# Step sizes of a selective-scan kernel: products of both halves in one instruction, both stores in slot 1

## The chip, the core and the metric

The kernel runs on one core of a Trainium2 chip. The core has TensorE (PE in the profile; PEld is its weight loads), VectorE (DVE), ScalarE (ACT), GpSimd (POOL), and SyncE (SP), which here only issues DMAs. The metric is the device time of one execution in microseconds. Three executions of the kernel before took 18705.48 to 18734.97 us, median 18718.93.

## What is computed

The input is 8 images of 48 x 48 pixels and 96 channels. Four layers follow each other, each in the form x = x + layer(group_norm(x)). Layer 0 and layer 3 are two-dimensional selective scans (`ss2d`), layer 1 is a spectral up- and downsampling with a small network between, layer 2 is a selective scan along lines (rows and columns, forwards and backwards). The scan that layers 0, 2 and 3 share, cut to what matters:

```python
delta = softplus(dts + dt_bias)                        # step sizes, 192 channels
def step(h, inp):                                      # along the sequence
    dl, u, B, C = inp
    dA = exp(dl[..., None] * A)                        # 16 states for each channel
    h = h * dA + (dl * u)[..., None] * B[:, None, :]
    return h, einsum('bdn,bn->bd', h, C)
```

Each layer scans every image in four directions (`k`). In layers 0 and 3 a sequence is all 48 x 48 pixels. In layer 2 each row or column of 48 is a sequence of its own. The product `dl * u` is what the change is about: it is called the step size product below.

## The kernel before, in words

The 192 channels are two halves of 96 (`DH`). An image and direction is cut into five blocks of rows, four of 480 pixels and one of 384 (`BLKS`). There are 160 blocks (8 images, 4 directions, 5 blocks) in each of the three scan layers.

For each block a first stage (`stage1`) makes u, the step sizes dt and the step size products du on 96 partitions. They stand in one SBUF tile, `dds`, as [96, half, dt or du, columns]. The pool has one such buffer. The scan itself works on 128 partitions, each a pair of 32 channels and 4 states, so dt and du have to be repeated. This goes through DRAM: `store_dd` (line 437, one DMA of 360 KB for a half) writes them to DRAM, and `load_dd` (line 219, one DMA of 1440 KB for a half) reads them back with each row going to four partitions. B and C take the same way: `bcl` is stored as `bcd` (line 812 in lines, 658 in `ss2d`) and read by `load_bc` (line 231, 480 KB each, four for a block, seven buffers). All these DMAs are issued by SP, in order; a DMA whose wait is not over holds up all that stand behind it.

A block of the scan has eight slots, two in each of four turns. In a turn DVE does three scans (line 298) and up to two products of du and B (line 266); POOL does the rest of those products (line 266) and the products of the states with C (line 304). ACT makes the exponentials (line 290) and copies B to PSUM for DVE (`copy_b`, line 247, one PSUM buffer). PE sums over the states (lines 320 to 326). Half 0 of du is needed first by the product for slot 0, which DVE does in the fourth turn of the block before.

The order on each engine is the order in which the program records instructions, which is written out by hand in `scans`. The first-stage steps of a block are put at slots before it: `stage1` returns a table of slot offsets, and `plan` adds to it the start of the block two before the one they are for. `aside(at)` runs at each slot: first the loads of the next block (`LOAD_BC` = slots 2, 3, 6, 7; `LOAD_DD` = slot 3 for half 0 and slot 5 for half 1), then one step of other work, then the first-stage steps of that slot. In the lines layer the table has the convolution at offsets 3 and 4, u at 6, `bcl` at 7, the softplus and the store of `bcd` at 8 (`s6`), the step size products at 9 (`s7`), the store of half 0 at 10 (`s8`) and of half 1 at 11. Offsets 8 to 11 are slots 0 to 3 of the block before the one they are for. In `ss2d` the products stand at offset 7 and the stores at 8 and 9, that is, slots 0 and 1.

So in the lines layer SP issues, for each block: `bcd` store (slot 0), `bc` load (slot 2), store of half 0 (slot 2), `bc` load, load of half 0 and store of half 1 (slot 3), load of half 1 (slot 5), two `bc` loads (slots 6 and 7). Below, store 0 and store 1, load 0 and load 1 are those of the two halves.

`make_du` makes the step size product of one half on POOL (line 452). It then marks the ends of sequences: in the lines layer by a memset of dt at each line's first pixel (line 455), one for each half; in `ss2d` by two memsets over both halves (lines 459 and 460), made with half 0.

Of the kernel before, what the change touches and what calls it, by code (L numbers as in the profile page):

```python
# [23 lines left out]
SEG = 48  # L24
# [15 lines left out]
FAR = 1e30  # L40
# [17 lines left out]
def rows(t, n):  # L58

    return t[:, :n].rearrange("p (r s) -> p r s", s=SEG)  # L60
# [37 lines left out]
def vss_stack_kernel(ctx: ExitStack, tc: tile.TileContext, i: dict, out: bass.AP):  # L98
    nc = tc.nc
# [336 lines left out]
    def store_dd(b, half):  # L436
        nc.sync.dma_start(b.dd[half].rearrange("j (g m) -> g j m", g=3), b.dds[:, half].rearrange("p t m -> p (t m)"))

    def sizes(b, half):

        return [b.dds[:, half, n, b.at] for n in range(2)]

    def make_room(b, pools):
        b.room = pools["dds"].tile([DH, LEAD + 4 * WMAX], F32, tag="dds", name="dds")
        b.dds = b.room[:, LEAD:LEAD + 4 * b.m].rearrange("p (h t m) -> p h t m", h=2, t=2)

    def make_du(b, half, u):


        n = b.n  # L450
        dt, du = sizes(b, half)
        nc.gpsimd.tensor_mul(rows(du, n), rows(dt, n), u)  # L452
        if b.m == b.n:
            at = SEG - 1 if b.rev else 0
            nc.gpsimd.memset(rows(dt, n)[:, :, at:at + 1], FAR)
        elif half == 0:

            far = b.dds[:, :, :, b.came:] if b.back else b.room[:, :4 * b.m].rearrange("p (u m) -> p u m", m=b.m)[:, :, :LEAD + 1]
            nc.gpsimd.memset(b.dds[:, :, :, 0:1] if b.back else b.dds[:, :, :, b.goes:], 0.0)
            nc.gpsimd.memset(far, FAR)  # L460


    def ss2d(l, xin, xout, b0=0):
# [169 lines left out]
        def stage1(b):  # L633
            n = b.n
            u = b.view(us[b.job], dirs[b.k][0])
            got = {}

            def raw(half):
                got["p"] = ps("s1", 1)
                nc.tensor.matmul(got["p"][:DH, :n], lhsT=dtw[2 * NS:, b.k, half, :], rhs=b.bcl[2 * NS:, :n],  # L640
                                 start=True, stop=True)

            def biased(half):
                nc.scalar.activation(sizes(b, half)[0], got["p"][:DH, :n], AF.Identity,  # L644
                                     bias=w[f"{l}_dtb"][:, b.k, half:half + 1])

            def s0():
                got["p"] = ps("s1", 1)
                for half in range(2):
                    nc.tensor.matmul(got["p"][:NBC, :n], lhsT=w[f"{l}_xp"][:, b.k, half, :], rhs=u[:, half],  # L650
                                     start=(half == 0), stop=(half == 1))

            def s1():
                b.bcl = pools["bcl"].tile([NBC, BMAX], F32, tag="bcl", name="bcl")
                nc.scalar.copy(b.bcl[:, :n], got["p"][:NBC, :n])

            def s3():
                nc.sync.dma_start(b.bcd, b.bcl[:2 * NS, :n])
                raw(0)

            def s4():
                make_room(b, pools)
                biased(0)
                raw(1)

            def s6():
                both = b.dds[:, :, 0, b.at]
                nc.scalar.activation(both, both, AF.Softplus)  # L668

            def du():  # L670
                for half in range(2):
                    make_du(b, half, u[:, half])

            def store(half):
                return lambda: store_dd(b, half)

            return {-1: s0, 1: s1, 3: s3, 4: s4, 5: lambda: biased(1), 6: s6, 7: du,
                    NG: store(0), NG + 1: store(1)}

# [27 lines left out]
    def lines(xin, xout):  # L707
# [24 lines left out]
        for k in range(NK):  # L732
            nc.vector.tensor_mul(taps[:, k], taps[:, k], wl["l2_inu"][:, k].unsqueeze(1).to_broadcast([DH, 4, 2 * DH]))
            for half in range(2):
                nc.scalar.activation(diag[:, k, half, :], wc["ident"], AF.Identity, scale=w["l2_d"][:, k, half:half + 1])

                p = ps("s1", 2)
# [12 lines left out]
        def shift(t, dy, dx):  # L750

            at = (pad + dy) * step + pad + dx
            return t[:, at:at + H * step].rearrange("p (h w) -> p h w", w=step)[:, :, :W]
# [10 lines left out]
        def stage1(b):  # L764
            n = b.n
            col, rev = dirs[b.k]
            xp = xpads[b.job % 2]
            got = {}

            def shifted(off):  # L770
                v = shift(xp, off, 0).rearrange("p h w -> p w h") if col else shift(xp, 0, off)
                return v[:, b.r0:b.r0 + b.nr, :]

            def conv(half):
                def run():
                    got["u", half] = ps("s1", 2)
                    for tap in range(4):
                        off = tap - 3 if not rev else 3 - tap
                        at = ((b.k * 4 + tap) * 2 + half) * DH
                        nc.tensor.matmul(got["u", half][:, :n], lhsT=flat[:, at:at + P],  # L780
                                         rhs=shifted(off), start=(tap == 0), stop=(tap == 3))
                return run

            def s2():
                b.ub = up.tile([DH, 2, BMAX], F32, tag="ub", name="ub")
                for half in range(2):
                    nc.scalar.activation(b.ub[:, half, :n], got["u", half][:DH, :n], AF.Silu,
                                         bias=w["l2_cb"][:, b.k, half:half + 1])

            def s2s3():  # L790
                s2()
                s3()

            def s3():
                got["p"] = ps("s1", 2)
                for half in range(2):
                    nc.tensor.matmul(got["p"][:NBC, :n], lhsT=w["l2_xp"][:, b.k, half, :], rhs=b.ub[:, half, :n],
                                     start=(half == 0), stop=(half == 1))

            def s4():  # L800
                b.bcl = pools["bcl"].tile([NBC, BMAX], F32, tag="bcl", name="bcl")
                nc.scalar.copy(b.bcl[:, :n], got["p"][:NBC, :n])  # L802

            def s5():
                s4()
                for half in range(2):
                    got[half] = ps("s1", 2)
                    nc.tensor.matmul(got[half][:DH, :n], lhsT=dtw[2 * NS:, b.k, half, :], rhs=b.bcl[2 * NS:, :n],  # L808
                                     start=True, stop=True)

            def s6():
                nc.sync.dma_start(b.bcd, b.bcl[:2 * NS, :n])
                make_room(b, pools)
                for half in range(2):
                    nc.scalar.activation(sizes(b, half)[0], got[half][:DH, :n], AF.Softplus,  # L815
                                         bias=w["l2_dtb"][:, b.k, half:half + 1])

            def s7():
                for half in range(2):
                    got["z", half] = ps("s1", 2)  # L820
                    nc.tensor.matmul(got["z", half][:DH, :n], lhsT=w["l2_inz"][:, b.k, half * DH:(half + 1) * DH],  # L821
                                     rhs=shifted(0)[:C], start=True, stop=True)
                for half in range(2):
                    make_du(b, half, rows(b.ub[:, half], n))

            def s8():
                b.zb = up.tile([DH, 2, BMAX], F32, tag="zb", name="zb", bufs=2)
                for half in range(2):
                    nc.scalar.activation(b.zb[:, half, :n], got["z", half][:DH, :n], AF.Silu)
                store_dd(b, 0)  # L830

            return {3: conv(0), 4: conv(1), 6: s2s3, 7: s5, 8: s6, 9: s7, 10: s8, 11: lambda: store_dd(b, 1)}

        def opening(b, half):
            return diag[:, b.k, half, :], b.ub[:, half, :b.n]
# [42 lines left out]
        for _ in front(0):  # L878
            pass
        scans(dirs, range(NK), True, ON_POOL_L2, a, pools, ps, stage1, opening, done, side, tail)  # L880
        stack.close()

# [287 lines left out]
```

## Time and profile before

| | |
|---|---|
| median of 3 executions | 18718.93 us |
| the profiled execution | 18722.42 us |
| its span, first to last instruction | 18720.7 us |
| DVE busy | 16219.3 us (87%) |
| POOL busy | 15238.6 us (81%) |
| PE busy | 14799.0 us (79%) |
| ACT busy | 13661.6 us (73%) |
| DMA, mean | 152 GB/s |
| step size products (line 452), 480 columns, `ss2d` | 512 of 1237 ns |
| the same, lines | 256 of 1031 ns |

The layers follow each other in time: the first `ss2d` up to about 5.5 ms, the spectral layer to about 7.0 ms, the lines layer from there to about 13.2 ms (its first step size product starts at 7070.7 us, its last at 13195.7), and the second `ss2d` to the end. Shares of busy time over the whole span mix these. In the stretch 1000 to 5300 us (`ss2d`) DVE is busy 4134.6 us of 4300 and POOL 4021.2; in 7300 to 12300 (lines) DVE 4463.6 of 5000 and POOL 4086.2; in 13500 to 18300 (`ss2d`) DVE 4611.1 of 4800 and POOL 4487.5.

A line of the timeline has the start in us, the duration in us, the engine, the source line, the operation, what is written and read, the shape, how many instructions were merged into the line, and in brackets the idle time before it and what ended it. SPq is SP's queue: its lines are the issues of DMAs, not their transfers.

### The profile page before, as it was taken

The page shows a single profiled execution, that of the slowest core. Times are in us where ns is not written, and L with a number is a line of the kernel's source. Part 1 is how long each engine was busy: PE and PEld are TensorE (multiplying, and loading weights), DVE is VectorE, ACT ScalarE, POOL GpSimd, SP SyncE. Part 2 cuts the span into 40 slices and gives each one's busy share as a digit, 9 for nine tenths or more (in the row PEclk, how much of TensorE's full clock was granted, in tenths as well). Part 3 has the DMA queues.
Part 4 walks back from the last instruction along what each step waited for, and adds up shares of the span by engine and source line. Part 5 has one row for each costly group of instructions (what it writes and reads, how often), then busy time and mean ns, then how long its engine had stood idle before and what let it go on. Part 6 is the DMA issues. An engine that isn't in the chain of part 4 may idle for free.

```text
span 18720.7 us, 168607 instructions
## 1 busy us (share of the span) xinstructions
PE 14799.0 (79%) x53500; PEld 4319.5 (23%) x53500; DVE 16219.3 (87%) x10329; ACT 13661.6 (73%) x20342; POOL 15238.6 (81%) x8639
## 2 busy tenths in 40 slices
PE   6777777777778887887888878878777777777777
PEld 1211211212215552222222222221121121121221
DVE  7999999999992218889898888888799999999998
ACT  6877877887772227777777777777687788778776
POOL 7999999999980008888888888888799999999998
PEclk7876787777767778888888888888677778778776
DMA  4544544544544334444444444343454554554444
GB/s 139 174 173 166 175 171 165 178 170 165 176 148 55 46 60 144 147 146 149 148 147 148 146 151 148 142 150 135 144 172 170 172 171 168 171 172 170 169 172 147
DMA packets 768455, 2836.52 MB, mean 152 GB/s; under 512 B 235724, under 2 KB 298668, under 8 KB 640926
## 3 DMA queue, kind: packets, MB, share of 16 engines
q1 hardware_dynamic: 767558, 2825.75, 45.0%
q8 instruction: 418, 6.85, 0.1%
q14 instruction: 479, 3.92, 0.1%
HBM read 2377.32 MB, written 448.17 MB: 151 GB/s over the span
## 4 chain that ended last, share of the span: by engine, by line
POOL 29%; DVE 16%; DMA 16%; PE 15%; issue 14%; ACT 9%; SPq 1%; POOLq 0%; DVEq 0%; ACTq 0%
POOL dbu L304 20%; DVE dbu L298 10%; DMA dd<-dds 8%; POOL dbu L266 6%; DMA bc<-bcd 6%; DVE dbu L266 4%; ACT ps_da L290 4%; PE ps_y L324 2%; POOL dds L452 2%; PE ps_h L1010 2%; PE ps_s L780 2%; PE ps_y L1023 2%; ACT L290 1%; PE ps_side L515 1%; PE ps_a L1000 1%
## 5 line engine op out<-in xcount | busy, mean ns | idle before, releaser
L298 DVE TENSOR_TENSOR_SCAN dbu<-ps_da,dbu 128x968 f32<-128x968 f32 (+3 forms) x5760 | 11814.6, 2074 | 615.1 <-ACT ps_da L290 511.7
L304 POOL TENSOR_TENSOR dbu<-dbu,bc 128x1440 f32<-128x1440 f32 (+1 forms) x3840 | 10062.3, 2633 | 1549.8 <-DVE dbu L298 1485.6
L290 ACT ACTIVATE ps_da<-dd,w_l_a 128x484 f32<-128x484 f32 (+3 forms) x11520 | 7429.8, 649 | 2970.4 <-DVE dbu L298 2732.3
L324 PE MATMUL ps_y<-dbu,w_red 128*32 128x480 f32 (+1 forms) x23040 | 4855.5, 736 | 2059.7 <-POOL dbu L304 2037.3
L326 PE MATMUL ps_y<-dbu,w_red 128*32 128x480 f32 (+1 forms) x7680 | 4814.4, 736 | 0.0
L266 DVE TENSOR_TENSOR dbu<-dd,ps_b 128x962 f32<-128x962 f32 (+5 forms) x2880 | 3831.1, 1330 | 387.8 <-ACT ps_b L247 353.1
L266 POOL TENSOR_TENSOR dbu<-dd,bc 128x481 f32<-128x481 f32 (+5 forms) x2240 | 3911.1, 1761 | 245.4 <-DMA bc<-bcd 136.7
L324 PEld LDWEIGHTS ps_y<-dbu,w_red 128*32 128x32 f32 x23040 | 743.5, 124 | 6084.7 <-POOL dbu L304 4390.8
L247 ACT COPY ps_b<-bc 128x482 f32<-128x482 f32 (+3 forms) x2720 | 1450.8, 533 | 463.4 <-DMA bc<-bcd 345.4
L780 PE MATMUL ps_s<-xpad,w_l_cw 128*128 128x480 f32 (+1 forms) x2560 | 1748.0, 835 | 2.2 <-ACT xpad L146 1.9
L515 PE MATMUL ps_side<-xpad,w_l_cw 128*128 128x480 f32 (+1 forms) x2880 | 1575.3, 676 | 17.7 <-ACT u L528 12.7
L290 ACT ACT_TABLE_LOAD x986 | 1265.0, 1283 | 17.4
L135 POOL MEMSET w_l_cw<- 128x1760 f32 (+1 forms) x3 | 5.8, 1941 | 1338.8 <-DVE x L990 1333.3
L320 PE MATMUL ps_y<-ysum,w_ident 96*96 96x480 f32 (+1 forms) x960 | 747.1, 867 | 285.7 <-ACT ysum L692 285.7
L452 POOL TENSOR_TENSOR dds<-dds,u 96x480 f32<-96x480 f32 (+1 forms) x640 | 764.7, 1195 | 207.2 <-ACT dds L668 181.6
L640 PE MATMUL ps_s<-bcl,dtw 6*96 6x480 f32 (+1 forms) x1280 | 867.0, 765 | 65.1 <-ACT dds L644 57.7
L650 PE MATMUL ps_s<-u,w_l_xp 96*38 96x480 f32 (+1 forms) x1280 | 843.4, 790 | 20.9 <-ACT z L530 17.9
L808 PE MATMUL ps_s<-bcl,dtw 6*96 6x480 f32 (+1 forms) x640 | 459.1, 859 | 500.1 <-ACT bcl L802 500.1
L515 PEld LDWEIGHTS ps_side<-xpad,w_l_cw 128*128 128x128 f32 x2880 | 581.7, 225 | 1067.7 <-issue 928.3
L780 PEld LDWEIGHTS ps_s<-xpad,w_l_cw 128*128 128x128 f32 x2560 | 513.9, 206 | 1070.0 <-issue 964.6
L326 PEld LDWEIGHTS ps_y<-dbu,w_red 128*32 128x32 f32 x7680 | 682.8, 124 | 0.0
L821 PE MATMUL ps_s<-xpad,w_l_inz 96*96 96x480 f32 (+1 forms) x640 | 504.0, 921 | 63.8 <-ACT dds L815 48.2
(147 smaller groups left out, 11829.0 us busy)
## 6 DMA issues: line engine op xcount, KB each, us to landing
dd<-dd SPq DMA_DIRECT2D x512, 1452.0 KB
bc<-bcd SPq DMA_DIRECT2D x1536, 480.0 KB
dd<-dd SPq DMA_DIRECT2D x256, 1440.0 KB
dd<-dds SPq DMA_DIRECT2D x512, 363.0 KB
dd<-dd SPq DMA_DIRECT2D x128, 1164.0 KB
bc<-bcd SPq DMA_DIRECT2D x384, 384.0 KB
dd<-dds SPq DMA_DIRECT2D x256, 360.0 KB
dd<-dd SPq DMA_DIRECT2D x64, 1152.0 KB
```

What stands on the lines that cost most here:

```text
L247: nc.scalar.copy(bps[t][:, :bcs[t][0].shape[1]], bcs[t][0])
L266: engine.tensor_mul(o, du, by.unsqueeze(1).to_broadcast([P, hi - lo, by.shape[1]]))
L290: nc.scalar.activation(da[:, at:at + b.m], b.got[half][:, u % 3, 0, :], AF.Exp, scale=a[:, b.k, ci:ci + 1])
L298: nc.vector.tensor_tensor_scan(db, da, db, 0.0, ALU.mult, ALU.add)
L304: nc.gpsimd.tensor_mul(h, h, bcs.pop(2 * t + sub)[1].unsqueeze(1).to_broadcast([P, 3, n]))
L324: nc.tensor.matmul(y[32 * g:32 * g + 32, :n], lhsT=wc["red"][:, :32], rhs=hc[:, g, b.at], start=False, stop=(slot == 3))
L326: nc.tensor.matmul(y[DH:, :n], lhsT=wc["red"][:, 32:], rhs=hc[:, 2, b.at], start=(slot == 0), stop=(slot == 3))
L452: nc.gpsimd.tensor_mul(rows(du, n), rows(dt, n), u)
L515: nc.tensor.matmul(pu[:, :n], lhsT=flat[:, at:at + P], rhs=xpad[:, r0 + dy:r0 + dy + nr, dx:dx + W], start=(tap == 0), stop=(tap == 8))
L640: nc.tensor.matmul(got["p"][:DH, :n], lhsT=dtw[2 * NS:, b.k, half, :], rhs=b.bcl[2 * NS:, :n], start=True, stop=True)
L650: nc.tensor.matmul(got["p"][:NBC, :n], lhsT=w[f"{l}_xp"][:, b.k, half, :], rhs=u[:, half], start=(half == 0), stop=(half == 1))
L780: nc.tensor.matmul(got["u", half][:, :n], lhsT=flat[:, at:at + P], rhs=shifted(off), start=(tap == 0), stop=(tap == 3))
```

## The change

`make_du` no longer takes a half. It multiplies both halves in one POOL instruction over [96, 2, rows, 48], in all three scan layers. In the lines layer the memset that marks the sequence starts becomes one for both halves as well; in `ss2d` the two memsets now follow the one product, where they stood between the two. In the lines layer both stores go to offset 9, right behind the products: SP issues them ahead of the `bc` loads of slots 2 and 3. The step `s8` keeps the gate's activation alone, and offset 11 is gone. In `ss2d` the stores stay at offsets 8 and 9.

```diff
-    def make_du(b, half, u):
-        n = b.n
-        dt, du = sizes(b, half)
-        nc.gpsimd.tensor_mul(rows(du, n), rows(dt, n), u)
+    def make_du(b, u):
+        dt, du = [b.dds[:, :, n, b.at].rearrange("p h (r s) -> p h r s", s=SEG) for n in range(2)]
+        nc.gpsimd.tensor_mul(du, dt, u)
         if b.m == b.n:
             at = SEG - 1 if b.rev else 0
-            nc.gpsimd.memset(rows(dt, n)[:, :, at:at + 1], FAR)
-        elif half == 0:
+            nc.gpsimd.memset(dt[:, :, :, at:at + 1], FAR)
+        else:
...
             def du():
-                for half in range(2):
-                    make_du(b, half, u[:, half])
+                make_du(b, u)
...
-                for half in range(2):
-                    make_du(b, half, rows(b.ub[:, half], n))
+                make_du(b, b.ub[:, :, :n].rearrange("p h (r s) -> p h r s", s=SEG))
+                for half in range(2):
+                    store_dd(b, half)
 
             def s8():
...
-                store_dd(b, 0)
...
-            return {3: conv(0), 4: conv(1), 6: s2s3, 7: s5, 8: s6, 9: s7, 10: s8, 11: lambda: store_dd(b, 1)}
+            return {3: conv(0), 4: conv(1), 6: s2s3, 7: s5, 8: s6, 9: s7, 10: s8}
```

## The prediction

> **What bounds the kernel now.** I read the stretches by stage first, then the chain of waits and SP's waits inside the lines stage, then one block of that stage on SP, POOL and DVE. The two `ss2d` stages keep DVE 96% and POOL 93 to 94% busy (4134.6 and 4021.2 of 4300 us between 1000 and 5300), the lines stage only 89% and 82% (4463.6 and 4086.2 of 5000 us between 7300 and 12300): it waits for something else. This is its chain, and the largest row of SP's waits in that stretch:
>
> ```profile
> by line: DMA dd<-dds 21.3%; DMA bc<-bcd 14.4%; issue 8.7%; DVE dbu L298 8.5%; PE ps_s L780 5.9%; ACT ps_da L290 5.4%; POOL dbu L304 4.6%; DVE dbu L266 3.2%; PE ps_y L324 3.1%; PE ps_s L852 2.4%; DMA x<-x 2.3%; ACT L290 2.1%; POOL dbu L266 2
> ```
>
> ```profile
> SPq L219 <- DMA dd<-dds: 2487.9, 263, 11.3
> ```
>
> Every one of the 263 loads of step sizes waits, 9.5 us on average, for its own store to land. One block on SP's queue, and what came of it on DVE and POOL:
>
> ```profile
> 8999.86 0.31 SPq L812 DMA_DIRECT2D bcd<-bcl  x1
> 9001.50 0.51 SPq L231 DMA_DIRECT2D bc<-bcd  x1
> 9008.11 0.74 SPq L437 DMA_DIRECT2D dd<-dds  x1
> 9008.90 0.54 SPq L231 DMA_DIRECT2D bc<-bcd  x1
> 9019.06 0.51 SPq L219 DMA_DIRECT2D dd<-dd  x1
> 9019.67 0.73 SPq L437 DMA_DIRECT2D dd<-dds  x1
> 9031.00 0.53 SPq L219 DMA_DIRECT2D dd<-dd  x1
> 9031.58 1.24 SPq L231 DMA_DIRECT2D bc<-bcd  x2
> ```
>
> ```profile
> 9026.54 1.62 DVE L266 TENSOR_TENSOR dbu<-dd,ps_b 128x1440 f32<-128x1440 f32 x1
> ...
> 9039.10 1.66 DVE L266 TENSOR_TENSOR dbu<-dd,ps_b 128x1440 f32<-128x1440 f32 x1 [3.12 <-ACT ps_b L247]
> ```
>
> ```profile
> 9006.88 1.03 POOL L452 TENSOR_TENSOR dds<-dds,ub 96x480 f32<-96x480 f32 x1
> 9007.97 0.11 POOL L455 MEMSET dds<- 96x10 f32 x1
> 9008.03 1.03 POOL L452 TENSOR_TENSOR dds<-dds,ub 96x480 f32<-96x480 f32 x1
> ...
> 9045.68 0.86 POOL L452 TENSOR_TENSOR dds<-dds,ub 96x384 f32<-96x384 f32 x1
> ```
>
> Store 0 goes out at 9008.11, load 0 at 9019.06, store 1 behind it, load 1 at 9031.00, and only then the last two loads of `bc`. The first of them lands at 9038.42 (by the trace's semaphore updates), ACT copies it, and DVE's slot-2 product starts at 9039.10 after 3.12 us idle. From there 6.58 us run to the next block's products. So the cycle is 1.23 (product to store 0) + 30.31 (store 0 to that landing) + 0.68 + 6.58 = 38.80 us, the whole spacing. Over 124 steady 480-column blocks the spacing is 38.68 on average (37.6 to 40.3), over the 32 short ones 34.77.
>
> **The change in the lines stage.** SP's order becomes `bcd`, store 0, store 1, `bc`, `bc`, load 0, load 1, `bc`, `bc`. The built order confirms this, so "it does not do what it says" is no rival. `ss2d` already issues in nearly this order, and shows the prices:
>
> ```profile
> 3097.35 2.23 SPq L437 DMA_DIRECT2D dd<-dds  x2
> 3099.68 3.13 SPq L231 DMA_DIRECT2D bc<-bcd  x2
> 3107.18 0.51 SPq L219 DMA_DIRECT2D dd<-dd  x1
> ...
> 3112.14 0.52 SPq L219 DMA_DIRECT2D dd<-dd  x1
> ```
>
> Store 0 lands 9.8 us after its issue (load 0 goes out the moment it does), store 1 4.9 us later. The `bc` loads land at 16.1 and 17.3, load 0 at 20.8 us after store 0's issue; load 1 and the next `bc` at 24.4 and 25.5. Over 193 such full blocks load 0 lands at 20.4 to 22.9 us, mean 21.06; over 53 short ones at 18.0 in the median. Today in lines that is 17.5 (16.1 short). The reason is in what the queue does while a store runs alone:
>
> ```profile
> 9013.50:9017.50 4.00, 3.93 (x8) 1.39 (x9) 4.00 (x4) 3.94 (x7) 4.00 (x3) 1.00 0.17 59
> ```
>
> The last two columns are the share of the 16 DMA engines and GB/s: 0.17 is under three engines. The second store queues behind the first there, the two `bc` loads behind both, and load 0's part behind all four. [...]
>
> - *Product to store 0:* two 480-column products become one of 960. By POOL's rows (480: 1035 ns, 960: 1884, 1440: 2738) an element costs 1.77 ns and an instruction 0.18 us, so 1.88; with the gap, the memset and the issue (0.06 + 0.11 + 0.03) store 0 goes out 2.08 us after the product starts, not 1.23. [...]
> - *Load 0 to the next block's first DVE product:* 2.08 + 20.9 (a little under 21.06, since a store is 360 KB here and 363 there) + 0.1 = 23.1 us after the product starts. Today that DVE product comes at 21.0 on average, for other reasons (load 0 landed 2.3 earlier): a new stall of about 2 us.
> - *From there to the next block's step size product:* today 17.66 on average, with the `bc` stall in it. That stall goes: `bc` would land at 2.08 + 25.5 = 27.6 and be wanted at 23.1 + 9.4. Without waits it is 9.5 (smallest seen to the slot-2 product) + 6.6 = 16.1.
> - *Spacing:* 23.1 + 16.1 = 39.2 against 38.68: +0.52 x 128 blocks = +67 us. For load 0 at 20.4 and 16.0 it is 38.6 (-13 us); for 16.93, the median of the 42 blocks that have no `bc` stall today, 40.0 (+170 us).
> - *Short blocks:* 1.74 + 18.0 + 0.1 = 19.8, and the product comes at 20.3 today anyway: 0, at most +0.3 x 32 = 10.
> - *What queues behind the stores:* the first `bc` load moves from 5.4 us before the product to behind both stores and lands at about 18.4. Its ACT copy (today at 16.4) comes 2 us later; what hides that is load 0, which comes later still. If load 0 came early, this copy would be next, at about 19.
> - *POOL's own saving here* (one fixed part, a memset, a gap; some 0.3 us a block) costs and gives nothing: POOL waits 709.5 us for DVE's scans in this stretch. PE, ACT and DVE get the same instructions in the same order.
>
> **The change in ss2d.** Only the merge. A block saves one fixed part, 0.18 us; the two memsets stay. POOL's lines hold 32.2 + 9.5 + 2.6 = 44% of the chain there, so of 320 x 0.18 = 58 us I take 26; the ends are 0 (DVE is the bound: it waits for POOL in about 36 of 4300 us) and 58. Store 0 goes out 0.85 to 1.25 us later, since it now waits for both halves. In the block above load 0 lands at 3118.11 and the DVE product that needs it starts at 3129.55, so 11 us hide that: 0.
>
> **Sum.** 67 - 26 = +41 us. The profiled execution took 18722.4 (span 18720.7, 1.7 around it), 3.5 above the median 18718.9; so 18763 there, 18760 as a median. What can be told from no change here is about 0.2%, 37 us.
>
> **The rivals.**
> - *The wait moves and costs more* (chance 0.20): after the later DVE product the path takes 16.93, as in the 42 rows without `bc` stall, because the scan after it waits 1.07 us for ACT, and ACT for PE's second convolution. +170 - 26: 18865. For it: nearly all those rows. Against: in them the convolution ends 5 us after that product, and with the product 2 us later it should end in time.
> - *Faster* (0.12): load 0 comes as early as today, because the second store and the two `bc` loads do not hold its share up. Then the product stays at 21.0 and only the `bc` stall goes: 21.0 + 16.93 = 37.9, -0.75 x 128 = -96, with the merge -122: 18597. It decides at load 0 landing 20.4 us after store 0; later is slower. For it: that is only half a microsecond from my price. Against: of 193 blocks in `ss2d` none is below 20.36.
> - *The two parts cancel* (0.11): POOL's saving counts in full (-58) and load 0 is at the early end (+20): 18680.
> - *My forecast* (0.57): 18760, its own range 18710 to 18810.
>
> Slower by over 0.2%: 0.28 of the forecast and the first rival, 0.48. Within: 0.27 + 0.08 = 0.35. Faster: 0.02 + 0.12 + 0.03 = 0.17. The range 18650 to 18900 leaves out the faster rival and little else: low is both favourable ends together (-13 - 58), high the first rival without any gain from the merge (18889) and 10 for the short blocks.
>
> **What would show it.** Right: stores 0.9 us apart, then two `bc`, load 0 about 9.8 and load 1 about 14.6 us after store 0; SP's waits for `dds` about half of 9.5 us each; DVE's wait for ACT's `ps_b` copies nearly gone, in its place some 2 us a block before the DVE product that reads load 0; spacing 39.2. POOL's product once a block at 1.88 us in lines, 1.9 to 2.7 in `ss2d`. Wrong: load 0 landing well under 20.4 us after store 0, or that DVE product starting long after the landing, or `ss2d` gaining much more than 26 us.

## The result and the profile after

The changed kernel takes 18672.24 us in the median (18661.37 to 18691.21) against 18720.53 for the kernel before beside it: a ratio of 0.9975, with an interval of 0.9966 to 0.9984. It is 48 us faster, where 18760 and most likely a slower kernel had been predicted. The profiled execution has a span of 18669.2 us against 18720.7.

Two figures of the section on the profile before are wrong: in the lines layer the first block's step size product starts at 6991.4 us and the last block's at 13017.6. The product at 13195.7 belongs to the second `ss2d` layer.

Where the 51.5 us between the two profiled executions lie shows when each scan layer is measured from the first scan of its first block to the first scan of its 160th (all times of this kind below are read so; the expectations count from product to product, which gives 6026.2 and 6034.7 for the lines layer):

| stage | before | after | difference |
|---|---|---|---|
| first ss2d layer | 5447.7 | 5425.0 | -22.7 |
| lines layer | 6020.5 | 6031.5 | +11.0 |
| second ss2d layer | 5449.8 | 5416.0 | -33.8 |
| all else | 1802.7 | 1796.7 | -6.0 |

The lines layer did get slower, by a sixth of what was forecast; the ss2d layers gained twice what was forecast. First the lines stage. This is its chain of waits after, between 7300 and 12300 us, and the row of SP's waits that the prediction showed for before:

```profile
by line: DMA dd<-dd 23.5%; issue 13.3%; DVE dbu L298 12.3%; DMA dd<-dds 8.2%; DVE dbu L266 6.9%; ACT ps_da L290 5.3%; ACT L290 4.4%; POOL dbu L304 3.7%; POOL dbu L266 2.4%; ACT L813 1.8%; POOL dds L451 1.7%; ACT dds L813 1.7%; PE ps_y L324 
```

```profile
SPq L219 <- DMA dd<-dds: 1119.9, 263, 5.6
```

The loads `dd<-dd` have taken the largest share of the chain from the stores' landing and `bc`. SP's wait for the stores is 4.3 us a load instead of 9.5, as foreseen. The next lines are one 480-column block on SP, on POOL and on VectorE (DVE):

```profile
8984.73 1.57 SPq L437 DMA_DIRECT2D dd<-dds  x2
8986.40 3.40 SPq L231 DMA_DIRECT2D bc<-bcd  x2
8994.39 5.19 SPq L219 DMA_DIRECT2D dd<-dd  x2
```

```profile
8982.63 1.88 POOL L451 TENSOR_TENSOR dds<-dds,ub 96x960 f32<-96x960 f32 x1
...
9021.24 1.55 POOL L451 TENSOR_TENSOR dds<-dds,ub 96x768 f32<-96x768 f32 x1
```

```profile
9005.38 1.65 DVE L266 TENSOR_TENSOR dbu<-dd,ps_b 128x1440 f32<-128x1440 f32 x1 [3.22 <-DMA dd<-dd]
```

Store 0 goes out 2.10 us after the product's start, load 0 9.66 us behind it, and by the trace's semaphore updates load 0 lands at 9005.29, 20.56 us after store 0. The VectorE product starts 0.09 us later, after 3.22 us idle, and 15.86 us after it the next block's step size product starts. In every long block behind the first the product starts 0.09 us after this landing. VectorE's waits in the whole stage say the same (total in us, times, longest):

```profile
DVE dbu L266 <- DMA dd<-dd: 270.6, 112, 5.0
...
DVE dbu L266 <- ACT ps_b L247: 0.2, 1, 0.2
```

The wait for ACT's `ps_b` copies (109.0 us before) is gone and one for load 0 has taken its place. So far this is the recorded mechanism. What it does not contain is in the ss2d layers. There the gain is not spread over the blocks. An image has 20 blocks in a layer, and the time from each block's first scan to the next one's is, in the mean over the images, 3.3 us (first layer) and 2.8 us (second) shorter in the ninth, 0.7 and 1.5 us in the tenth, and within 0.6 us of before in all others but the fifth (1.2 us longer, in the first layer only). In the ninth block the group norm of the next image takes its last small step, `shift = -gm * rs`, a VectorE instruction on 96 x 1 numbers. These are its six executions after 13500 us, before and after (ns: shortest, median, longest):

```profile
L183 DVE SCALAR_TENSOR_TENSOR shift<-gm,rs x6: 5896/5908/5937, 14192.2 to 17622.0; 96x1 f32<-96x1 f32 x6
```

```profile
L183 DVE SCALAR_TENSOR_TENSOR shift<-gm,rs x6: 156/164/5676, 14181.0 to 17584.1; 96x1 f32<-96x1 f32 x6
```

Before, a step on one number per partition took 5.9 us. This is the timeline of DVE and of POOL around one of them, before:

```profile
1788.03 0.12 DVE L181 RECIPROCAL rs<-rs 96x1 f32<-96x1 f32 x1
1788.18 5.92 DVE L183 SCALAR_TENSOR_TENSOR shift<-gm,rs 96x1 f32<-96x1 f32 x1
1794.03 2.16 DVE L298 TENSOR_TENSOR_SCAN dbu<-ps_da,dbu 128x968 f32<-128x968 f32 x1
```

```profile
1784.80 3.73 POOL L266 TENSOR_TENSOR dbu<-dd,bc 128x481 f32<-128x481 f32 x2
1788.48 0.19 POOL L278 COPY dbu<-dbu 128x5 f32<-128x5 f32 x1
1788.63 5.43 POOL L304 TENSOR_TENSOR dbu<-dbu,bc 128x1440 f32<-128x1440 f32 x2
1794.00 0.19 POOL L278 COPY dbu<-dbu 128x5 f32<-128x5 f32 x1
```

and after:

```profile
1787.02 0.13 DVE L181 RECIPROCAL rs<-rs 96x1 f32<-96x1 f32 x1
1787.18 0.17 DVE L183 SCALAR_TENSOR_TENSOR shift<-gm,rs 96x1 f32<-96x1 f32 x1
1788.06 2.17 DVE L298 TENSOR_TENSOR_SCAN dbu<-ps_da,dbu 128x968 f32<-128x968 f32 x1 [0.71 <-ACT ps_da L290]
```

```profile
1783.56 3.73 POOL L266 TENSOR_TENSOR dbu<-dd,bc 128x481 f32<-128x481 f32 x2
1787.25 0.18 POOL L278 COPY dbu<-dbu 128x5 f32<-128x5 f32 x1
1787.39 5.43 POOL L304 TENSOR_TENSOR dbu<-dbu,bc 128x1440 f32<-128x1440 f32 x2
```

Before, the step starts 0.35 us ahead of the end of a POOL instruction, and it ends only when three more have followed without a gap, 0.04 us after the second of the two L304. After, it starts 0.11 us ahead of that end and gets through at once. This is so in all 12 executions that fall in a ninth block before (5.90 to 5.94 us, starting 0.34 to 0.37 us ahead), and in 11 of 12 after (0.15 to 0.24 us, starting 0.08 to 0.12 us ahead); the twelfth, at 0.11 us, took 5.68. In the first image of each layer the step falls in an earlier block and takes 1.55 us in both kernels. This step reads `gm` and `rs` from SBUF, and it is held for 5.9 us and not only for the 0.35 us that the running POOL instruction still had. In the same 12 blocks before, the reciprocal just ahead of it (L181), which reads one operand from SBUF, starts 0.50 to 0.53 us ahead of that end and takes 0.12 to 0.13 us. The scans and products beside it read one operand from PSUM. That the second operand from SBUF is what makes the step wait is a reading of these rows; no run changes it alone.

### The profile page after: what moved, and what is told of

Its sections match the earlier page's. It is cut to its first block, busy times and chain, and to the rows that moved or that the text cites. A ratio compares the mean times of both kernels' runs of the same rounds, so it can differ in the third digit from the quotient of the medians.

```text
span 18669.2 us, 167485 instructions
## 1 busy us (share of the span) xinstructions
PE 14901.4 (80%) x53500; PEld 4322.6 (23%) x53500; DVE 16160.3 (87%) x10329; ACT 13662.4 (73%) x20342; POOL 15136.7 (81%) x7999
## 4 chain that ended last, share of the span: by engine, by line
POOL 27%; DVE 18%; issue 16%; DMA 15%; PE 13%; ACT 11%; SPq 0%; POOLq 0%; DVEq 0%; ACTq 0%
POOL dbu L304 17%; DVE dbu L298 11%; DMA dd<-dd 9%; POOL dbu L266 6%; DVE dbu L266 5%; ACT ps_da L290 4%; DMA dd<-dds 3%; POOL dds L451 3%; ACT L290 2%; PE ps_y L324 2%; PE ps_h L1008 2%; PE ps_y L1021 2%; DMA bc<-bcd 1%; PE ps_side L514 1%; PE ps_a L998 1%
## 5 line engine op out<-in xcount | busy, mean ns | idle before, releaser
L304 POOL TENSOR_TENSOR dbu<-dbu,bc 128x1440 f32<-128x1440 f32 (+1 forms) x3840 | 10062.5, 2633 | 1842.3 <-DVE dbu L298 1768.0
L290 ACT ACT_TABLE_LOAD x986 | 1265.0, 1283 | 17.5
L649 PE MATMUL ps_s<-u,w_l_xp 96*38 96x480 f32 (+1 forms) x1280 | 840.8, 788 | 20.4 <-ACT z L529 17.4
L451 POOL TENSOR_TENSOR dds<-dds,u 96x960 f32<-96x960 f32 (+1 forms) x320 | 706.8, 2209 | 183.9 <-ACT dds L667 183.9
L795 PE MATMUL ps_s<-ub,w_l_xp 96*38 96x480 f32 (+1 forms) x640 | 385.0, 738 | 304.4 <-ACT ub L785 304.4
```

The costliest lines, as they stand in the source:

```text
L290: nc.scalar.activation(da[:, at:at + b.m], b.got[half][:, u % 3, 0, :], AF.Exp, scale=a[:, b.k, ci:ci + 1])
L304: nc.gpsimd.tensor_mul(h, h, bcs.pop(2 * t + sub)[1].unsqueeze(1).to_broadcast([P, 3, n]))
L451: nc.gpsimd.tensor_mul(du, dt, u)
```

## The experiments

Two theories stood against each other for the ss2d layers: *the norm step*, as just described, and *GpSimd time*, the recorded one, by which 0.18 us less POOL work in each of 320 blocks counts, if need be in full (58 us). For the lines layer the question was what makes load 0 late. The table has all stage lengths, each from the one profiled execution of its run. Kernels with the same ss2d code differ by up to 17 us in the sum of the two layers (before, e2 and e9; after, e6, e7 and e8), so differences of that size are not read. The lines layer has 6013.3 to 6025.4 us where its code is that of before (e1, e3, e5, e12) and 6031.5 to 6032.8 where it is that of after (e2, e4).

| run | us (median) | ratio to before, interval | ss2d | lines | ss2d |
|---|---|---|---|---|---|
| before | 18712.67 to 18722.75 | | 5447.7 | 6020.5 | 5449.8 |
| after | 18672.24 | 0.9975 (0.9966 to 0.9984) | 5425.0 | 6031.5 | 5416.0 |
| e1 merge in ss2d alone | 18651.33 | 0.9967 (0.9955 to 0.998) | 5416.9 | 6025.4 | 5417.7 |
| e2 lines part alone | 18733.41 | 1.0008 (1.0 to 1.0017) | 5445.0 | 6032.4 | 5435.6 |
| e3 before, shift on ACT | 18663.8 | 0.9972 (0.996 to 0.9983) | 5420.3 | 6021.7 | 5416.8 |
| e4 after, shift on ACT | 18672.86 | 0.9978 (0.9968 to 0.9988) | 5413.6 | 6032.8 | 5421.7 |
| e5 before, products cut | 18819.27 | 1.0052 (1.0039 to 1.0064) | 5488.4 | 6013.7 | 5488.4 |
| e6 after, store behind its own product | 18572.14 | 0.9919 (0.9906 to 0.9933) | 5403.8 | 5936.2 | 5427.8 |
| e7 after, `bc` off the stores | 18445.98 | 0.9859 (0.9844 to 0.9874) | 5422.0 | 5807.2 | 5416.7 |
| e8 after, three-part store in lines | 18380.83 | 0.9818 (0.9805 to 0.9832) | 5422.0 | 5739.5 | 5425.0 |
| e9 before, three-part store in lines | 18409.8 | 0.9835 (0.9821 to 0.9848) | 5448.2 | 5721.0 | 5443.9 |
| e10 all together | 18204.07 | 0.9723 (0.9709 to 0.9736) | 5363.2 | 5720.8 | 5363.2 |
| e11 e10 without the ss2d stores | 18289.97 | 0.9769 (0.9755 to 0.9782) | 5401.0 | 5721.1 | 5402.2 |
| e12 before, three-part store in ss2d | 18700.84 | 0.9992 (0.9983 to 1.0001) | 5452.2 | 6013.3 | 5449.7 |

### e1 and e2: each part alone

```diff
 # e1, against before: ss2d's du() calls the merged make_du, lines keeps two
-                for half in range(2):
-                    make_du(b, half, u[:, half])
+                make_du(b, u)
```

> The kernel before with the one-instruction product in the two ss2d layers alone; the lines layer is as before. Both theories of the gain put it into the ss2d layers, where the traces of before and after differ by -22.6 and -30.9 us: both expect about -54 us against the kernel before, that is 18667 us, with the lines stage at 6026 us as before. They differ in how it gets there. 'The norm step' (the group norm's small VectorE step shift<-gm,rs stood up to 5.9 us behind a run of GpSimd instructions, and the merged product moves that run): the gain sits in one of the 20 blocks of an image, where that step runs, and its 32 executions take about 29 us in sum instead of 82. 'GpSimd time' (0.18 us less of GpSimd work in each of 320 blocks, which counts in full because GpSimd sets the pace): the gain is spread over all blocks, 0.17 us in each.

```diff
 # e2, against after: ss2d's du() keeps two products
-                make_du(b, u)
+                for half in range(2):
+                    make_du_half(b, half, u[:, half])
```

> The kernel before with the lines layer's part alone: merged product and both stores in slot 1; the ss2d layers with two products as before. If the parts add up, the lines stage takes 6035 us instead of 6026 (+8.5 us, the 480-column blocks +0.24 us each, the 384-column blocks -0.7 us each) and the ss2d layers stay at 5435 and 5437: 18729 us. If the recorded prediction's pricing of this part was right and the profiled run hid it (a phase), the sum is +67 us: 18787 us. Below 18700 us the early stores would be a gain of their own.

The merge alone gives -64.6 us, the lines part +17.5 (its interval begins at no change at all), which together is the change's -48 within what the runs can tell. In e1 the lines stage is as before (+4.9), and the two ss2d layers lose 30.8 and 32.1 us. Of the mean 3.9 and 4.0 us that an image loses, the ninth and tenth block have 4.1 and 4.4; the other 18 blocks together are 0.2 and 0.4 us longer. The same six executions of the step in e1, and then in e2:

```profile
L183 DVE SCALAR_TENSOR_TENSOR shift<-gm,rs x6: 156/162/179, 14168.4 to 17574.9; 96x1 f32<-96x1 f32 x6
```

```profile
L183 DVE SCALAR_TENSOR_TENSOR shift<-gm,rs x6: 5907/5914/5921, 14197.0 to 17614.7; 96x1 f32<-96x1 f32 x6
```

With the merge the step is short, without it long, in all 12 ninth blocks of each run. GpSimd's 0.18 us per block, over all blocks, is not to be seen. But e1 does not yet say that the step costs the time; it could be a sign of something else that the merge moves.

### e3 and e4: the step taken away, with and without the merge

```diff
-        nc.vector.tensor_copy(gm, got["p"][:C, :1])
+        nc.vector.tensor_scalar(gm, got["p"][:C, :1], -1.0, None, ALU.mult)
...
-        nc.vector.tensor_sub(dev, mv[:, 0:1], gm)
+        nc.vector.tensor_add(dev, mv[:, 0:1], gm)
...
-        nc.vector.scalar_tensor_tensor(shift, gm, -1.0, rs, ALU.mult, ALU.mult)
+        nc.scalar.activation(shift, gm, AF.Identity, scale=rs)
```

> The kernel before, products and stores untouched; only the group norm's shift = -mean/deviation is computed on ScalarE (an activation with the reciprocal as its scale) instead of by the small VectorE instruction with two SBUF inputs. 'The norm step': that instruction's 82 us of VectorE time go, of which about 75 lie in the two ss2d layers and on VectorE's path, so -45 to -75 us: 18645 to 18675 us, the gain in the same block of each image as in the changed kernel. 'GpSimd time': nothing that GpSimd does is changed, so within 10 us of before: 18710 to 18730 us.

> The changed kernel with the same shift on ScalarE. 'The norm step': in the changed kernel this instruction costs little in ss2d (one execution of 5.7 us is left, the others take 0.2 us), and 2.7 us each in seven executions of the lines layer, where VectorE waits for load 0 anyway: 0 to -15 us against the changed kernel, 18657 to 18672 us, and against run e3 the merge in ss2d is then worth nothing (within 10 us). 'GpSimd time': the merge keeps its worth of 54 us beside e3, that is 18672 us here and 18720 us there.

On ACT the step takes 0.29 us. With products and stores as before, e3 is 52 us faster than before (18663.8 against 18715.94), and again the ninth block of an image loses 3.1 us in both layers. That is the whole gain of the change, had by moving one small step and without the merge. With the step on ACT the merge is worth nothing: the two ss2d layers take 10837.1 us in e3 and 10835.3 in e4, and e4 (18672.86) is not faster than the changed kernel. So the norm step is the cause of the gain.

What this does not separate is the merge's saving of POOL work from its later store 0. Between 500 and 5400 us VectorE waits 0.5 us for load 0 in e3 and 5.9 in e4, between 13600 and 18500 us 0.5 and 8.1. So the saving may be worth nothing, or some 13 us that the later store takes back (an estimate from these four waits).

### e5: more work for POOL

```diff
 # e5, against before; make_du takes the rows to multiply as a new argument
                 for half in range(2):
-                    make_du(b, half, u[:, half])
+                    dt, du = [rows(v, n) for v in sizes(b, half)]
+                    nc.gpsimd.tensor_mul(du[:, :3], dt[:, :3], u[:, half, :3])
+                    nc.gpsimd.tensor_mul(du[:, 3:5], dt[:, 3:5], u[:, half, 3:5])
+                    make_du(b, half, u[:, half], slice(5, None))
```

> The kernel before with each of the two step size products of an ss2d block cut into three (3, 2 and the remaining rows): the same elements, four GpSimd instructions more in each of 320 blocks, 0.18 us each by the difference between one long and two short products, so 0.72 us of GpSimd work per block. 'GpSimd time': if GpSimd's 0.18 us counted in full or at the recorded prediction's 44 per cent, four times as much must cost +100 to +230 us, evenly over the blocks: 18820 to 18950 us. 'The norm step': GpSimd has room in these blocks and the time hangs on where the norm's step falls; the two ss2d layers change by -55 to +20 us, in one or two positions of an image: 18660 to 18740 us.

This run went against what the theory that won in e3 and e4 expected of it. Between 500 and 6000 us the products take 350.3 us of POOL before, and in this run:

```profile
L452 POOL TENSOR_TENSOR dds<-dds,u 96x240 f32<-96x240 f32 (+1 forms) x294 | 195.6, 665 | 0.0
L673 POOL TENSOR_TENSOR dds<-dds,u 96x144 f32<-96x144 f32 x294 | 146.1, 497 | 5.9
L674 POOL TENSOR_TENSOR dds<-dds,u 96x96 f32<-96x96 f32 x294 | 115.1, 391 | 0.0
```

which is 106.5 us more in 147 blocks, 0.72 each, as worked out. The kernel is 102 us slower by the medians, and the ss2d layers 40.7 and 38.6 us in the profiled execution, which is the fastest of the five (18796.24). The loss is spread over most blocks: 0.25 us a block by the profile and 0.32 by the medians, a third to under a half of what was added. So POOL's time does count in ss2d once there is more of it, while the merge, which takes 0.18 us away, gave nothing (e1, e4). If some 0.4 to 0.5 us of POOL's work per block is covered (0.72 less 0.25 or 0.32; an estimate from this one run), both readings fit. So they do if the later store 0 takes the saving back. A run with a smaller addition, which would show the bend, was not made.

### e6, e7, e8: what makes load 0 late in lines

```diff
 # e6, against after, in lines
-                make_du(b, b.ub[:, :, :n].rearrange("p h (r s) -> p h r s", s=SEG))
                 for half in range(2):
+                    make_du_half(b, half, rows(b.ub[:, half], n))
                     store_dd(b, half)
```

> The changed kernel, but in the lines layer two products again, each with its memset and its store right behind it, both in slot 1 (ss2d keeps the merge). Theory 'load 0 is the wait': store 0 goes out 1.2 us behind the first product's start instead of 2.09, load 0 and the VectorE product that waits for it come 0.86 us sooner in the 127 long blocks: lines stage 6035 - 109 = about 5926 us, total 18563 us; VectorE's wait for load 0 shrinks from 2.4 to about 1.6 us a block. Rival 'the stage has another pace' (transfer volume, GpSimd, ScalarE): lines stays at 6025 to 6045 us, total about 18672 us.

```diff
 # e7, against after
-                if slot in LOAD_BC:
-                    load_bc(NG * nblk + LOAD_BC.index(slot))
+                at_slots = (1, 4, 6, 7) if restart else LOAD_BC
+                if slot in at_slots:
+                    load_bc(NG * nblk + at_slots.index(slot))
```

> The changed kernel, but in the lines layer the first bc load goes out ahead of the two stores (slot 1) and the second behind load 0 (slot 4), so that no bc load stands between the stores and load 0. If the two bc loads take their time on the engines that the stores use, load 0 lands 1.2 us (one bc load's 0.49 MB over 16 engines) to 2.4 us sooner than 20.67 us after store 0; VectorE waits as much less, 127 long blocks: 150 to 290 us less, 18380 to 18520 us. Rival: load 0 is held by the two stores alone, or bc, now late, takes over the wait: VectorE's wait moves from load 0 to ScalarE's ps_b copies, 18620 to 18720 us.

```diff
 # e8, against after, in store_dd
+        o, i = b.dd[half].rearrange("j (g m) -> g j m", g=3), b.dds[:, half].rearrange("p t m -> p (t m)")
+        if b.m == b.n:
+            for g in range(3):
+                nc.sync.dma_start(o[g], i[32 * g:32 * g + 32])
+        else:
+            nc.sync.dma_start(o, i)
```

> The changed kernel, but in the lines layer each store is three DMAs of 32 rows each instead of one of 96 rows seen as [3, 32, ...]: same bytes, same places. If a store is slow because its outermost dimension of 3 puts it on three of 16 DMA engines, each now spreads over 16, the store lands 3 to 5 us behind its issue instead of 9.7, load 0 lands 12 to 16 us behind store 0 instead of 20.67, and VectorE no longer waits for it: 2.4 us of 127 blocks, about -300 us, 18370 us, if nothing else (the second product, bc, GpSimd) is late next; half of it if something is. If the number of engines is not what holds the store, the store still lands about 9 us behind its issue and the time stays within 40 us of 18672, or grows by the four more DMAs on SP.

In e6 store 0 goes out 1.23 us behind its product instead of 2.09, load 0 lands 20.77 us behind it (20.67 in the changed kernel), and the 127 long blocks go from 38.93 to 38.18 us. The lines stage loses 95 us, the kernel 100; the total is within 10 us of the expectation. In this layer the merge is a loss, since it holds store 0 back for the second half. Against the kernel before, e6's lines layer is 84 us shorter: the early stores by themselves gain, and the merge takes that back.

In e7 the stores land as late as ever, 9.66 us after store 0's issue, so the `bc` loads do not slow the stores. They slow load 0, which queues behind them: it now lands 18.32 us after store 0, 2.35 earlier. The lines stage loses 224 us. VectorE's waits for load 0, in e6 and then in e7, over the same stretch as above (270.6 in the changed kernel):

```profile
DVE dbu L266 <- DMA dd<-dd: 205.9, 102, 4.3
```

```profile
DVE dbu L266 <- DMA dd<-dd: 35.6, 45, 3.4
```

In e8 one store is three DMAs of 32 rows. By the semaphore updates each part lands 1.9 to 2.4 us after its issue in the mean over the long blocks, and the whole of store 0 2.9 us after its first part goes out, instead of 9.7. The next lines are one short block of e8 on SP, and what the 16 DMA engines do while nothing but these parts runs (the last two columns are their share and GB/s; the same view before had 0.17 and 59 with a store alone):

```profile
8918.68 2.65 SPq L440 DMA_DIRECT2D dd<-dds  x6
8921.44 1.17 SPq L231 DMA_DIRECT2D bc<-bcd  x2
8922.77 1.94 SPq L219 DMA_DIRECT2D dd<-dd  x2
```

```profile
8919.50:8921.30 1.80, 1.57 (x8) 0.09 (x8) 1.80 (x2) 1.32 (x2) 1.80 (x1) 0.64 0.90 208
```

Load 0 goes out 4.1 us after store 0 and lands, over the long blocks, 12.8 us after it, 5.4 us ahead of its use; VectorE waits for no load any more. The lines stage loses 292 us, the kernel 291, as expected. That a 96-row store seen as [3, 32, ...] sits on three engines, the condition in the expectation of e8, is what its remedy bears out: the share of 0.90 is 14.4 of the 16 engines, where 0.17 is 2.7. The semaphore updates agree. Each of the 320 stores of 96 rows in the changed kernel's lines layer gets one update about 1.15 us after its issue and then just three, each of the 960 parts in e8 gets 16. Every load gets 16 as well. Of load 0's, thirteen have come 15.8 us after store 0 in the mean, and the last only at 20.1 (over all blocks): the part of load 0 that is late is three sixteenths of it, which fits the three engines that the stores hold.

### e9: the same store without the change

```diff
 # against before: the same store_dd as in e8, nothing else
```

> The kernel before, products and order of the stores untouched, with each store of the lines layer cut into three DMAs of 32 rows, as in run e8. If the three engines behind the 96-row store were what set the cycle of before (store 0 to the late bc landing, 30.31 of 38.80 us), this alone takes the lines stage to about 5740 to 5760 us as in e8, and the total to 18410 to 18450 us, 54 us above e8 at most for the ss2d layers' norm step: then the place of the stores is worth little once they are wide. If the late issue of store 1 (behind load 0) and of the last bc loads holds the cycle as well, the lines stage stays above 5850 us and the total above 18530 us.

With wide stores the old order gives 5721.0 us in lines, 18.5 less than e8: the place of the stores, which the change is about, is then worth little, and what is left of the difference seems to be the norm again. In lines the norm's steps L171, L172, L173 and L183 take 39.5 us of VectorE in e8 and 12.0 in e9, where they happen to fall better. They take 39.7 in the changed kernel, where the wait for load 0 covers the shift at least: e4, with the shift on ACT, is no shorter in lines. Run e11, which is e8 with those steps on ACT, has 5721.1. The counterpart, e9 with those steps on ACT, was not made.

### e10, e11, e12: the best of it, and a surprise taken apart

```diff
 # e10, against after: three-part store in all scan layers; shift as in e4, and
-        nc.vector.tensor_sub(dev, mv[:, 0:1], gm)
-        nc.vector.tensor_mul(dev, dev, dev)
-        nc.vector.tensor_add(dev, dev, mv[:, 1:2])
+        off = small.tile([C, 1], F32, tag="off", name="off")
+        nc.scalar.activation(off, mv[:, 0:1], AF.Identity, bias=gm)
+        dev = small.tile([C, 1], F32, tag="dev", name="dev")
+        nc.scalar.activation(dev, off, AF.Identity, scale=off, bias=mv[:, 1:2])
 # e11, against e10: three-part store in lines alone
 # e12, against before: three-part store in ss2d alone
```

> The changed kernel with the three-part store in all scan layers, and with all small steps of the group norm that read two SBUF operands (mean minus group mean, its square plus the variance, shift) on ScalarE. 'The norm step' extended: in ss2d the subtraction and the square still take 0.7 and 1.4 us each instead of 0.15 on VectorE (14 norms in the two layers and around them), of which two thirds lie on the path as with the shift: 15 to 25 us less than run e8, 18355 to 18370 us; the wide stores give nothing in ss2d, where 11 us hide them. Rival: those steps fall into VectorE's waits, or the two ScalarE steps cost as much on the exponentials' engine: 18375 to 18395 us, as e8.

> Run e10 without its three-part stores in ss2d: the changed kernel with three-part stores in lines alone, and the group norm's small steps on ScalarE. Run e10 came out 177 us under e8, where 15 to 25 were expected, and it joins two edits. If the norm steps are the cause, this run keeps most of it: 18200 to 18260 us. If the stores of ss2d are (not hidden after all), it keeps only the norm steps' 15 to 40 us: 18340 to 18366 us, the gain in positions 7 and 8 of an image.

> The kernel before with the three-part store in the two ss2d layers alone; products, lines layer and norm as before. The recorded prediction says that the ss2d store has 11 us to spare: then nothing, 18705 to 18735 us. If the rest of e10's surprise sits in these stores (or in what queues behind them on the DMA engines), this run is 60 to 140 us under before: 18580 to 18660 us, spread over many blocks of ss2d.

e10 came out at 18204.07 us, some 150 us under what was expected, and is the fastest kernel of this study: 2.8% under the one before. e11 and e12 take it apart, and neither expectation for e11 was met. The norm steps on ACT are worth 91 us beside e8 (18380.83 to 18289.97), four times the 15 to 25 expected. In the profiled executions, which lie 74.5 us apart, it is 21.0 and 22.8 us in the ss2d layers, 18.4 in lines, and 15.6 between the first ss2d layer and the lines layer, where the spectral layer runs its own norms, which the expectation had left out. It had also read two rows too small: in ss2d the subtraction (L171) takes 1.3 to 1.8 us and the square (L172) 2.66 in each of the 14 norms beside the scans, not 0.7 and 1.4. The ss2d stores are worth 86 us more on top of that, 37.8 and 39.0 of them in the two layers, yet on the kernel before (e12) 12 us (32 at most by the interval) and nothing within the ss2d layers. So the recorded sentence that 11 us hide those stores holds for the kernel before, and no longer in e11, which has the merge and is without the slow norm steps and the waits in lines. One thing that changes is POOL's wait for `bc` in the first ss2d layer (500 to 5400 us). It stands here for e11 and then for e10:

```profile
POOL dbu L304 <- DMA bc<-bcd: 29.3, 19, 3.6
```

```profile
POOL dbu L304 <- DMA bc<-bcd: 0.5, 1, 0.5
```

VectorE's waits for load 0 go as well, 8.2 us in e11 and none in e10. But the kernel before has 19.4 us of POOL's wait and e12 6.2, without a gain. The two pairs also differ in the merge: the kernel before has two products in ss2d, with store 0 earlier, and its VectorE waits 0.3 us for load 0. Why the same edit gives 77 us in the one and nothing in the other stays open.

## Why the prediction was wrong

Between the forecast of +41 us and the -51.5 us of the two profiled executions lie 92.5 us: 56 in the lines term (+67 forecast, +11.0 measured), 30.5 in the ss2d term (-26 and -56.5), and 6.0 in the rest, which the sum left out. The first is a wrong size, the second a wrong mechanism.

- **The step whose mechanism failed** is the ss2d term: "POOL's lines hold 32.2 + 9.5 + 2.6 = 44% of the chain there, so of 320 x 0.18 = 58 us I take 26." The saving is real (a product of 960 takes 2292 ns instead of 2 x 1237), but beside e3 the merge is worth nothing (e4). What it did bring, 56 to 63 us in the two layers (after, e1), came by a mechanism that the prediction does not have: a 0.2 us VectorE step that stood behind POOL for 5.9 us in twelve places. The step now starts 0.11 instead of 0.35 us ahead of the end of a POOL instruction. Nothing in the change aimed at that quarter of a microsecond, so that the step fell on the good side is luck. The term's end of 0, argued from VectorE being the bound, is where the merge came out without the step; but the 96% that VectorE was busy counted the blocked step as its work. The row was there to be read, among the groups of the profile before:

```profile
L183 DVE SCALAR_TENSOR_TENSOR shift<-gm,rs 96x1 f32<-96x1 f32 x32 | 82.0, 2564 | 1.1
```

- **The lines term was mis-sized.** Its mechanism and sign were right, +67 forecast against +11.0 by scans (+8.5 by products). Load 0 landed 20.67 us after store 0 (20.9 forecast), the VectorE product came 22.87 us after the step size product (23.1) and the next one 16.04 after that (16.1), so the long spacing is 38.93 instead of 39.2: +0.24 us on 127 blocks, 30 us. The other half of the miss is the short blocks, forecast at 0: they lost 0.69 us each, 22 us in 32. Their VectorE product comes 19.93 us after the step size product instead of 20.29, and the path behind it takes 14.15 us instead of 14.48; what makes either shorter was not traced. A term that is the small difference of two long paths (39.2 and 38.68) turns on tenths: 0.3 us in the spacing is half of it.
- *The details named as signs* came as written: stores 0.9 us apart (0.84), load 0 about 9.8 us after store 0 (9.7), SP's waits halved, the `ps_b` wait gone, some 2 us before the product that reads load 0 (2.55 against 0 before), POOL's product at 1.88 us. "`ss2d` gaining much more than 26 us" stood among the signs of a wrong prediction, and is what happened.
- *Store 0 of ss2d later at no cost:* not quite. In the changed kernel VectorE waits 7.2 us for load 0 in each of the stretches 500 to 5400 and 13600 to 18500 us, before 0.3 and 0.8. What this costs by itself was not measured; e12, where the wide store gives nothing, starts from the kernel before and has the early store.
- *The two parts cancel*, 18680: its time is the nearest of the four, but its reason is not. It took POOL's saving in full and load 0 at the early end, and neither was so. Its +20 us is not worked out either: 20.4 us with the path of 16.1 gives 38.68, which is no change.
- *Faster*, 18597: its point was load 0 at 20.4 us after store 0. It landed at 20.67, and no gain came from there. *The wait moves and costs more*, 18865: the path behind the VectorE product took 16.04 us, not 16.93.

## What to carry to other kernels

Look in the groups for instructions that take far longer than their size. Here a VectorE step on one number per partition, reading two SBUF operands, took 5.9 us instead of 0.16 because it stood behind GpSimd. Moving it to ScalarE was worth as much as the whole change (e3), and all three such steps of the norm 91 us beside wide stores (e11). A gain that sits in one block out of twenty is not the gain of an edit that touches every block, so cut the difference by position before believing a cause. And before a transfer is moved to an earlier place, look at how many DMA engines it uses: the same bytes in three pieces of 32 rows landed 2.9 instead of 9.7 us after they went out, and that was worth 16 times what the lines part of the change cost (e8, e2).

## What the runs showed of the hardware that was not expected

- The shift step, which reads two SBUF operands on VectorE, was held for more than the GpSimd instruction that ran. In the ninth blocks it was passed over by three more GpSimd instructions that followed without a gap: 5.9 us when it started 0.34 to 0.37 us before the end of the first (12 of 12 before, 12 of 12 in e2). It got through at that end when it started 0.08 to 0.12 us before (11 of 12 after, 12 of 12 in e1).
- Elsewhere in the same kernel one instruction is all that held such a step. The subtraction L171 starts 1.3 to 1.8 us before the end of a GpSimd instruction in all 14 norms beside the scans of ss2d, takes 1.3 to 1.8 us, and is let in at that end although the next GpSimd instruction follows at once. What decides at these boundaries is not shown by any run.
- In lines the two `bc` loads behind the stores in the queue did not delay the stores at all (9.66 us with and without them, e7), but delayed the load behind them by 2.35 us.
- GpSimd work in ss2d cost a third of its length or somewhat more when added (0.25 to 0.32 of 0.72 us a block), and the merge, which takes 0.18 us away but sends store 0 later, gave nothing.
